# First attention of a two-layer transformer: values in two halves, each behind its half of the rounds, and keys and values of the next group half an iteration later

## The chip, the core and the metric

The kernel runs on one core of a Trainium2 chip. The metric is the device time of one execution in microseconds (us). Engines are named as in the profile: PE is TensorE's matmul stream and PEld its weight loads, DVE is VectorE, ACT is ScalarE, POOL is GpSimd, SP issues most DMAs. Everything is fp32.

## What is computed

64 sequences `x` of 128 rows and width 128 go through two blocks of attention and experts, each with a residual sum:

```python
x = x + xattn0(layernorm(x), fside, ctx, ctx, ...)   # keys: 128 of fside @ Wk, and 120 raw ctx rows
x = x + ffn0(layernorm(x), wqkv, w1, w2)             # top 2 of 8 experts, attention router
x = x + xattn1(layernorm(x), ctx, ctx, ...)          # 120 keys
x = x + ffn1(layernorm(x), Wg, bg, W1, W2)           # top 2 of 8 experts

def xattn0(x1, x2, mem_k, mem_v, ...):               # 16 heads of 8
    q = x1 @ Wq + bq
    k = concat(x2 @ Wk + bk, mem_k); v = concat(x2 @ Wv + bv, mem_v)
    out = softmax(q k^T / sqrt(8)) v                 # per head, 248 keys
    return out @ Wp + bp
```

The first attention (`xattn0`) is the part that matters here: 64 x 16 heads of a 128 x 248 score matrix.

## The kernel before, in words

**Loops.** `attention()` (L232) is run once for each layer; `first` is true for the first. It is a software pipeline over `it` = 0 to 68 (L553): in one iteration different sequences stand at different stages. `on(back, f)` runs a step for sequence `it - back`. In the first attention, iteration `it` does:

1. `rounds(0, 1)`: in each round two banks of row maxima for sequence `it` (`max_bank`, matmuls L394, then a DVE reduction L414) and two banks of transposed scores for sequence `it - 2` (`score_bank`, L430, then an exp on ACT, L438). All 32 matmuls of a pair of rounds work on 32 rows of the PE array, four at a time. Rounds 0 and 1 take the maxima of heads' half 0 and the scores against the 128 computed keys; rounds 2 and 3 the maxima of half 1 and the scores against the 120 context keys.
2. `out4` (output projection, L511, of `it - 5`), `shift` (two transposes L459 of the maxima of `it - 1`, and two DVE operations L462 that put them into the queries), `out5` (residual sum L516 and statistics L109).
3. `aside.ahead` (statistics of a later sequence) and `aside.call`: the router of the first experts, which works for two groups at a time in small pieces. One `call` is made here and one more ahead of the second pair of rounds. Its pieces are DVE operations (L718 to L774, L820 to L861), some on ACT and POOL, and on PE transposes (L176), logits (L681, copied by DVE in L685) and counts (L831, which waits for DVE's L820).
4. `values(it - 3, 0)`, `values(it - 3, 1)` and `out1`: probabilities times values, L475, on 32 columns of the PE array; each half is 16 matmuls (32 records in the profile, as each fp32 matmul has two). Both halves write one bank, and `out1` copies its 256 columns (ACT, L484).
5. `context` (in one iteration of four), `prep(it, 0)`, the second `aside.call`.
6. `rounds(2, 3)`.
7. `out3` (transpose L504, ACT copy L506) of `it - 4`, `out2` (two transposes L491, then DVE's L495 and L497) of `it - 3`, `prep(it, 1)`, `aside.end` (DMAs of zeros, each behind L495).

**Groups.** Four sequences make a group; keys, values and queries are prepared for a whole group, one group ahead. With `j = it % 4`, `prep(it, half)` does:

- `j` = 0: `prep_q` in both halves. The matmul L292 and two ACT writes L301 come in half 0, two more writes from the same bank in half 1.
- `j` = 1: nothing. In these iterations the router has its transposes and logits on PE.
- `j` = 2: `prep_v` (four matmuls L214, DVE adds L221) in half 0, `prep_k` (matmul L202, two ACT writes L207) in half 1.
- `j` = 3: `prep_x` in half 1 (transposes L176, ACT copy L177).

`context` loads 2 x 240 KB of context keys (L261) and 960 KB of context values (L266) for the next group, into the slot of the group before. `prep_v` writes the values of that slot too, so both must come after the last `values` of the old group, which stand at `j` = 2.

**Order.** PE, ACT, DVE and POOL run in the order of the program text (`tc.manual_schedule(engines=ORDERED)`); only SP's queue is put in order by the planner.

**Banks.** `mtile()` takes one of eight PSUM banks. A new tile gets the bank that was given back first, and a bank is given back behind its last reader in program order. So the tile number n waits for the reader that gave back number n - 8. In a pair of rounds the order is maximum, score, maximum, score, for each round. A bank that is held over other work (that of `prep_q`, from half 0 to half 1) leaves seven for what comes between. The last bank of rounds 2 and 3 at `j` = 0 is therefore the first bank of the same pair, behind its reduction.

Of the kernel before, what the change touches and what calls it, by code (L numbers as in the profile page):

```python
# [8 lines left out]
F32 = mybir.dt.float32  # L9
# [9 lines left out]
GB = 4  # L19
NG = B // GB  # L20
S = 128
# [3 lines left out]
NV = 2  # L25
# [19 lines left out]
def transformer_kernel(ctx, tc, a, out):  # L45
    nc = tc.nc
# [46 lines left out]
    rows = ctx.enter_context(tc.tile_pool(name="rows", bufs=2))  # L93
# [91 lines left out]
    for s in range(2):  # L185
        k = keep.tile([128, NV, GB, KF + KC], F32, name=f"k2_{s}", tag=f"k2_{s}")
        K2.append(k)
        v = keep.tile([KF, GB, H // 2, 2, 32], F32, name=f"v_{s}", tag=f"v_{s}")
# [23 lines left out]
    def values_of(w, src, g, n0, pv):  # L212
        for j in range(GB):
            nc.tensor.matmul(  # L214
                pv[:n0, j * D : (j + 1) * D], lhsT=src[:, j, :], rhs=w["wv"],
                start=True, stop=True,
            )
        pv5 = pv[:n0, :].rearrange("k (b h i d) -> k b h i d", b=GB, i=2, d=HD)
        bv5 = w["bv"][:n0, :].rearrange("k (h i d) -> k h i d", i=2, d=HD)
        for i in range(2):  # L220
            nc.vector.tensor_tensor(  # L221
                VS[g % 2][0][:n0, :, :, i, 16 * i : 16 * i + HD], pv5[:, :, :, i, :],
                bv5[:, :, i, :].unsqueeze(1).to_broadcast([n0, GB, H // 2, HD]),
                ALU.add,
            )
# [6 lines left out]
    def attention(layer, w, norm, first, aside):  # L232
# [5 lines left out]
        with ExitStack() as es:  # L238
# [5 lines left out]
            if first:  # L244
                for s in range(2):
                    v = work.tile([128, GB, H // 2, 2, 32], F32, name="vc", tag="vc")
# [4 lines left out]
            src, q4s, xnTs, ps_, pavs, pts, ots, normed = {}, {}, {}, {}, {}, {}, {}, {}  # L251
# [7 lines left out]
            def context_k(g):  # L259
                for v in range(NV):  # L260
                    nc.sync.dma_start(  # L261
                        k2[g % 2][:, v, :, KF:], a["ctx_k"][:, v, g * GB : (g + 1) * GB, :]
                    )

            def context_v(g):
                nc.sync.dma_start(  # L266
                    vs[g % 2][1].rearrange("k b h i w -> k b (h i w)"),
                    a["ctx_v"][:, g * GB : (g + 1) * GB, :],
                )

            def context(g):
                if first:
                    context_k(g)
                    context_v(g)

            def mtile():
                return banks.tile([128, 512], F32, name="bank", tag="bank")
# [28 lines left out]
            def prep_k(g):  # L306
                keys_of(w, src[g], g, n0, mtile())
# [9 lines left out]
            def prep_v(g):  # L317
                values_of(w, src[g], g, n0, mtile())
# [20 lines left out]
            def prep(it, half):  # L339

                g, j = it // GB + 1, it % GB
                if not first:
                    if g == 1:
                        if (j, half) == (0, 0):
                            prep_k(1)
                            prep_v(1)
                        elif (j, half) == (0, 1):
                            prep_x(1)
                        elif j == 1:
                            prep_q(1, half)  # L350
                            if half:
                                prep_heads(1)
                    elif g < NG:
                        pieces = (
                            (), (lambda: prep_k(g), lambda: prep_heads(g)),
                            (lambda: prep_v(g), lambda: prep_x(g)),
                            (lambda: prep_q(g, 0), lambda: prep_q(g, 1)),
                        )[j]
                        if half < len(pieces):
                            pieces[half]()  # L360
                    return
                if half == 0 and it < GB - 1:
                    prep_batch(it + 1)
                if (it, half) == (0, 1):
                    prep_v(0)
                    norm_of(1)
                if (it, half) == (1, 1):
                    biased(0)
                if (it, half) == (2, 1):
                    prep_x(1)  # L370
                if (it, half) == (3, 0):
                    prep_q(1, 0)
                    prep_q(1, 1)
                if (j, half) == (3, 1):
                    if g + 1 < NG:
                        prep_x(g + 1)
                elif g >= NG:
                    return
                elif j == 0 and it:
                    prep_q(g, half)  # L380
                elif (j, half) == (2, 0):
                    prep_v(g)
                elif (j, half) == (2, 1):
                    prep_k(g)


# [78 lines left out]

            def values(b, v):
                g, j = divmod(b, GB)
                if v == 0:
                    pavs[b] = mtile()
                pav = pavs[b]  # L470
                p = ps_[b]
                for i in range(2):
                    for c, (_, n) in enumerate(chunks):
                        for ra in range(4):
                            nc.tensor.matmul(  # L475
                                pav[32 * ra : 32 * ra + 32, v * S : (v + 1) * S],
                                lhsT=vs[g % 2][c][:, j, 4 * v + ra, i, :],
                                rhs=p[:n, c, ra, (2 * v + i) * S : (2 * v + i + 1) * S],
                                start=(i == 0 and c == 0), stop=(i == 1 and c == nc_ - 1),
                            )  # L480

            def out1(b):
                ov = rows.tile([128, NV * S], F32, name="ov", tag="ov")
                nc.scalar.copy(ov, pavs.pop(b)[:, : NV * S])  # L484
                ots[b] = ov

            def out2(b):
                ov = ots.pop(b)
# [30 lines left out]
            def norm_of(g):  # L519
                if g < NG:  # L520
                    normed[g] = norm.normed(g)
                    biased(g)
# [30 lines left out]
            for it in range(B + 5):  # L553
                def on(back, *steps):
                    b = it - back
                    if 0 <= b < B:
                        for f in steps:
                            f(b)

                def rounds(*which):  # L560
                    ba = it if it < B else None
                    bc = it - 2 if 0 <= it - 2 < B else None
                    for r in which:
                        if ba is not None or bc is not None:
                            round_(ba, bc, r)

                if first and it % GB == 2:
                    norm_of(it // GB + 2)
                if 2 <= it <= B + 1 and it - 2 not in ps_:
                    ps_[it - 2] = work.tile([128, nc_, 4, 512], F32, name="p", tag="p")  # L570
                if it % GB == 0 and 0 < it // GB + 1 < NG:
                    if it:
                        loads(it // GB + 1)
                vals = (lambda b: values(b, 0), lambda b: values(b, 1), out1)
                if first:
                    rounds(0, 1)


                    on(5, out4)
                    on(1, shift)  # L580
                    on(5, out5)
                    aside.ahead(it)
                    aside.call(it, mtile)
                    on(3, *vals)
                    if it % GB == 2 and it // GB + 1 < NG:
                        context(it // GB + 1)
                    prep(it, 0)
                    aside.call(it, mtile)
                    rounds(2, 3)
                    on(4, out3)  # L590
                    on(3, out2)
                    prep(it, 1)
                    aside.end(it, work, mtile)
                else:
                    on(3, *vals)
                    rounds(0, 1)


                    aside.piece(mtile)
                    prep(it, 0)  # L600
                    on(4, out3)
                    on(3, out2)
                    on(5, out4)
                    aside.call(it, mtile)
                    prep(it, 1)
                    on(1, shift)
                    on(5, out5)
                    aside.ahead(it)
                    if it > GB and it % GB == 1:
                        norm_of(it // GB + 1)  # L610
                    aside.fetch_for(it)
                    aside.call(it, mtile)
                ps_.pop(it - 3, None)
                yield
# [951 lines left out]
```

## Time and profile before

| | |
|---|---|
| median of 3 runs | 1522.33 us (1518.69 to 1523.64) |
| profiled execution | 1516.1 us, of which 1514.3 us are the span of the trace |
| granted PE clock, mean | 0.989 |
| first attention's loop | about 20 to 615 us of the span |
| experts of the first layer, second attention with its experts | about 615 to 965 us, 965 to 1514 us |
| iterations 33 to 40, start of L459 to start of L459 | 320.0 to 394.9 us: 74.9 us for eight |

Work repeats every eight iterations, because the router takes two groups at a time. Times within the trace are from the start of the span. A line of the timeline has the start, the length, engine, line, operation, output and inputs, shapes, count, and in brackets the idle time of the engine ahead of it and what ended it. A line of the waits has who waited for whom, the sum in us, how often, and the longest.

### The profile page before, as it was taken

How to read it: one execution, taken by the hardware profiler on the slowest of the kernel's cores; microseconds unless marked ns; L12 is line 12 of the kernel's file. 1: busy time of each engine (PE TensorE's matmuls, PEld its weight loads, DVE VectorE, ACT ScalarE, POOL GpSimd, SP SyncE). 2: the span in 40 equal slices, each digit the busy share in tenths (PEclk: the TensorE clock that was granted, in tenths of full speed). 3: DMA queues.
4: the chain of work that ended last, by engine and by line, in shares of the span. 5: the costliest groups of instructions: out<-in, count | busy, mean ns of one | idle time of the engine just before them, and what ended most of it. 6: DMA issues, size and time to landing. Idle time of an engine off the chain costs nothing.

```text
span 1514.3 us, 42033 instructions
## 1 busy us (share of the span) xinstructions
PE 1421.0 (94%) x16620; PEld 1107.5 (73%) x16620; DVE 1102.4 (73%) x3024; ACT 847.6 (56%) x1740; POOL 640.4 (42%) x1195
## 2 busy tenths in 40 slices
PE   7999999999999999888999999898999999999987
PEld 5777777777777677777888888566666776767665
DVE  6777888888888988455754444687777778787763
ACT  4666666666666666543333333566667566666643
POOL 4123254646465635654001122377546555454210
PEclk9999999999999999999999999899999999999999
DMA  8433333333222221366766667111011111100000
GB/s 201 120 80 80 79 82 96 89 93 94 63 66 60 58 73 40 107 184 202 214 197 199 201 195 205 49 34 34 22 36 29 39 35 32 31 29 23 8 16 22
DMA packets 143719, 133.03 MB, mean 88 GB/s; under 512 B 48546, under 2 KB 126114, under 8 KB 141602
## 3 DMA queue, kind: packets, MB, share of 16 engines
q1 hardware_dynamic: 135330, 113.02, 27.3%
q0 software_dynamic: 8192, 17.32, 3.7%
q8 instruction: 132, 2.16, 0.6%
q14 instruction: 65, 0.53, 0.1%
HBM read 97.32 MB, written 32.97 MB: 86 GB/s over the span
## 4 chain that ended last, share of the span: by engine, by line
PE 69%; DVE 15%; DMA 4%; POOL 4%; ACT 4%; issue 2%; SPq 1%; POOLq 0%; DVEq 0%; ACTq 0%
PE bank L430 11%; PE bank L394 10%; PE bank L475 9%; PE bank L1115 9%; PE bank L1424 4%; PE bank L1445 4%; DVE nm L414 4%; PE bank L1128 3%; DMA q<-xs 2%; PE bank L407 2%; PE bank L214 2%; DVE q L462 2%; PE bank L511 2%; PE bank L681 2%; PE bank L202 2%
## 5 line engine op out<-in xcount | busy, mean ns | idle before, releaser
L414 DVE TENSOR_REDUCE nm<-bank 128x2 f32<-128x496 f32 (+1 forms) x768 | 463.5, 662 | 77.6 <-PE bank L430 61.8
L438 ACT ACTIVATE p<-bank 120x512 f32<-120x512 f32 (+1 forms) x768 | 402.1, 605 | 126.8 <-PE bank L430 123.9
L430 PE MATMUL bank<-q,k 32*120 32x256 f32 (+1 forms) x3072 | 438.1, 399 | 11.4 <-DVE nm L414 5.2
L430 PEld LDWEIGHTS bank<-q,k 32*120 32x120 f32 (+1 forms) x3072 | 293.5, 181 | 56.8 <-DVE nm L414 17.3
L394 PE MATMUL bank<-k,q 32*128 32x248 f32 x2048 | 291.0, 399 | 0.7 <-ACT q L334 0.5
L394 PEld LDWEIGHTS bank<-k,q 32*128 32x128 f32 x2048 | 202.2, 189 | 47.9 <-issue 11.0
L1120 DVE TENSOR_TENSOR p<-p,bank 128x256 f32<-128x256 f32 x213 | 88.0, 420 | 121.0 <-ACT p L1119 120.5
L475 PE MATMUL bank<-p,v 128*32 128x128 f32 (+1 forms) x4096 | 175.6, 275 | 0.2
L407 PE MATMUL bank<-k,qf 32*128 32x480 f32 x512 | 153.8, 602 | 0.8 <-ACT qf L295 0.8
L807 POOL DMA_INDIRECT xs<-xn,at x128 | 129.2, 1009 | 27.9 <-issue 24.3
L1119 ACT ACTIVATE p<-bank 128x256 f32<-128x256 f32 x213 | 81.0, 384 | 98.9 <-PE bank L1115 97.9
L484 ACT COPY ov<-bank 128x256 f32<-128x256 f32 x128 | 48.1, 376 | 143.5 <-PE bank L475 143.4
L475 PEld LDWEIGHTS bank<-p,v 128*32 128x32 f32 (+1 forms) x4096 | 108.8, 109 | 22.8 <-issue 13.7
L1364 POOL DMA_INDIRECT yb<-ys,back x112 | 108.5, 969 | 27.7 <-issue 19.5
L1115 PE MATMUL bank<-q 128*128 128x256 f32 x516 | 118.6, 379 | 1.6 <-ACT q L1106 1.6
L462 DVE SCALAR_TENSOR_TENSOR q<-bank,c_smask,q 128x256 f32<-128x256 f32 x256 | 111.1, 475 | 8.2 <-PE bank L459 7.8
L167 POOL TENSOR_SCALAR xn<-x,mv,rstd 128x128 f32<-128x128 f32 x252 | 110.2, 449 | 7.5 <-issue 1.4
L1115 PEld LDWEIGHTS bank<-q 128*128 128x128 f32 x516 | 94.7, 190 | 13.0 <-ACT q L1106 1.9
L475 PE MATMUL bank<-p,vc 120*32 120x128 f32 x2048 | 103.2, 272 | 0.0
L155 POOL TENSOR_SCALAR rstd<-mv 128x4 f32<-128x4 f32 x32 | 6.3, 198 | 219.9 <-DVE mv L113 123.0
L301 ACT ACTIVATE q<-bank,c_a_bq,c_hmask 128x512 f32<-128x512 f32 x124 | 90.1, 789 | 9.8 <-PE bank L292 9.8
L1157 POOL DMA_INDIRECT kvT<-ys,back x16 | 15.4, 961 | 189.7 <-DMA vc<-xs 114.0
(224 smaller groups left out, 2465.7 us busy)
## 6 DMA issues: line engine op xcount, KB each, us to landing
q<-in_w SPq DMA_DIRECT2D x43, 576.0 KB
vc<-in_w SPq DMA_DIRECT2D x28, 576.0 KB
vc<-in_ctx_v SPq DMA_DIRECT2D x16, 960.0 KB
ys<-zero SPq DMA_DIRECT2D x71, 128.0 KB
k<-in_ctx_k SPq DMA_DIRECT2D x32, 240.0 KB
q<-xs SPq DMA_DIRECT2D x43, 128.0 KB
ys<-q SPq DMA_DIRECT2D x43, 128.0 KB
x<-in_x SPq DMA_DIRECT2D x16, 256.0 KB
```

The source lines that it names most:

```text
L167: nc.gpsimd.tensor_scalar(xn[:, j, :D], xg[g][:, j, :], self.mv[:, b, 0:1], self.rstd[:, b : b + 1], ALU.add, ALU.mult,)
L301: nc.scalar.activation(q4s[g][:, :, s, :], pq.rearrange("p (b q) -> p b q", b=GB), AF.Identity, bias=w["bq"][:, s : s + 1], scale=hmask[:, ...
L394: nc.tensor.matmul(pa[:, u, :], lhsT=q4s[g][r, j, s, :], rhs=k2[g % 2][r, s // 2, j, :], start=True, stop=True,)
L407: lambda: nc.tensor.matmul(pa, lhsT=qfs[g][r, j, :], rhs=k4s[g][r, :, j, :], start=True, stop=True),
L414: nc.vector.tensor_reduce(nm[b % 2].rearrange("q i (a s) -> q a i s", s=16)[:, 2 * ra + v : 2 * ra + v + len(slots) // 2, :, 0], pa.rearra ...
L430: nc.tensor.matmul(pb[:n, v * 256 : (v + 1) * 256], lhsT=k2[g % 2][r, v, j, k0 : k0 + n], rhs=q4s[g][r, j, 2 * v : 2 * v + 2, :].rearrange ...
L438: nc.scalar.activation(ps_[b][:n, c, ra, :], pb[:n], AF.Exp, scale=SCALE)
L462: nc.vector.scalar_tensor_tensor(q, pm, smask[:, v : v + 1], q, ALU.mult, ALU.add)
L475: nc.tensor.matmul(pav[32 * ra : 32 * ra + 32, v * S : (v + 1) * S], lhsT=vs[g % 2][c][:, j, 4 * v + ra, i, :], rhs=p[:n, c, ra, (2 * v + ...
L807: s = nc.gpsimd.indirect_dma_start(xs, bass.IndirectOffsetOnAxis(at[:, j, k : k + 1], 0), xn, None)
L1115: nc.tensor.matmul(ph[:, u, :], lhsT=w[:, c, u * 128 : (u + 1) * 128], rhs=xT, start=True, stop=True)
L1364: nc.gpsimd.indirect_dma_start(y[:, k, b % 2, :], None, ys, bass.IndirectOffsetOnAxis(back[:, b, k : k + 1], 0),)
```

## The change

- `half_out(b, v)` computes one half of the values into a bank of its own and copies its 128 columns into the half of a common tile `ov`. Half 0 stands where the whole values stood, half 1 behind `rounds(2, 3)`. `out1` isn't used in the first attention any more.
- `context` and `prep_v` for the next group move behind half 1, `prep_k` moves from half 1 of `prep` into half 0, where `prep_v` was.
- `prep(it, 1)` moves ahead of `out2`, so that `prep_x`'s transposes and the second two writes of `prep_q` stand between `out3` and `out2`.

The second attention keeps its order.

```diff
@@ -379,8 +379,6 @@
                 elif j == 0 and it:
                     prep_q(g, half)
                 elif (j, half) == (2, 0):
-                    prep_v(g)
-                elif (j, half) == (2, 1):
                     prep_k(g)
@@ -465,7 +463,7 @@
             def values(b, v):
                 g, j = divmod(b, GB)
-                if v == 0:
+                if v == 0 or first:
                     pavs[b] = mtile()
@@ -483,6 +481,14 @@
+            def half_out(b, v):
+
+                values(b, v)
+                if v == 0:
+                    ots[b] = rows.tile([128, NV * S], F32, name="ov", tag="ov")
+                cols = slice(v * S, (v + 1) * S)
+                nc.scalar.copy(ots[b][:, cols], pavs.pop(b)[:, cols])
@@ -581,15 +587,17 @@
                     on(5, out5)
                     aside.ahead(it)
                     aside.call(it, mtile)
-                    on(3, *vals)
-                    if it % GB == 2 and it // GB + 1 < NG:
-                        context(it // GB + 1)
+                    on(3, lambda b: half_out(b, 0))
                     prep(it, 0)
                     aside.call(it, mtile)
                     rounds(2, 3)
+                    on(3, lambda b: half_out(b, 1))
+                    if it % GB == 2 and it // GB + 1 < NG:
+                        context(it // GB + 1)
+                        prep_v(it // GB + 1)
                     on(4, out3)
+                    prep(it, 1)
                     on(3, out2)
-                    prep(it, 1)
                     aside.end(it, work, mtile)
```

## The prediction

> **What bounds the kernel now.** I read the page first, then the stretches of 100 us, then the waits of the first attention, then the timelines of PE and DVE for a few of its iterations.
>
> ```profile
> PE 1421.0 (94%) x16620; PEld 1107.5 (73%) x16620; DVE 1102.4 (73%) x3024; ACT 847.6 (56%) x1740; POOL 640.4 (42%) x1195
> ```
> ```profile
> 300.00:400.00 100.00, 98.67 (x1545) 75.09 (x1543) 86.08 (x215) 65.15 (x132) 55.83 (x126) 1.00 0.30 80
> ```
> Columns of the second: length, then PE, PEld, DVE, ACT, POOL busy us, clock, DMA share, GB/s. In the first attention (20 to 615 us, the only place that the change touches) PE looks full at the full clock and DVE stands at 86%. The ends of matmuls are modelled, so I measured PE from start to start:
>
> ```profile
> 361.40 0.47 PE L394 MATMUL bank<-k,q 32*128 32x248 f32 x1
> ...
> 363.31 0.33 PE L504 MATMUL bank<-ident,o 128*128 128x128 f32 x1
> ```
> ```profile
> 326.14 0.47 PE L394 MATMUL bank<-k,q 32*128 32x248 f32 x1
> ...
> 328.91 0.38 PE L511 MATMUL bank<-c_a_wo,oT 128*128 128x128 f32 x1
> ```
> Both are the same 32 matmuls. A pair of rounds that waits for nothing takes 363.31 - 361.40 = 1.91 us; the other takes 2.77. Call rounds 0 and 1 the first pair, 2 and 3 the second, and `it` mod 4 the position. From 100 to 500 us the first pair takes 2.77, 2.66, 2.41, 2.96 at positions 2, 3, 0, 1, so it stalls 0.86 + 0.75 + 0.50 + 1.05 = 3.16 us in each four iterations; the second is clean except at position 0 (2.92) and 2 (2.03 to 2.09). The waits name the cause:
>
> ```profile
> DVE nm L414 <- PE bank L430: 42.8, 84, 2.0
> PEld bank L504 <- DVE nm L414: 14.4, 37, 2.4
> PEld bank L430 <- DVE nm L414: 14.4, 36, 1.6
> ```
> PE waits for banks that DVE's reductions give back, and DVE in its turn waits for PE: eight banks tie two nearly full engines together. DVE between two pairs:
>
> ```profile
> 346.93 1.83 DVE L414 TENSOR_REDUCE nm<-bank 128x2 f32<-128x496 f32 x3
> 348.67 0.87 DVE L462 SCALAR_TENSOR_TENSOR q<-bank,c_smask,q 128x256 f32<-128x256 f32 x2
> 349.46 0.28 DVE L516 TENSOR_TENSOR x<-x,bank 128x128 f32<-128x128 f32 x1
> 349.77 0.49 DVE L109 BATCH_NORM_STATS2 st<-x 128x6 f32<-128x128 f32 x2
> 350.18 0.22 DVE L841 COPY flat<-counts 128x64 f32<-128x64 f32 x1
> ...
> 351.31 0.23 DVE L855 TENSOR_TENSOR row<-row,start 128x64 f32<-128x64 f32 x1
> 352.21 1.26 DVE L414 TENSOR_REDUCE nm<-bank 128x2 f32<-128x496 f32 x2 [0.67 <-PE bank L430]
> 353.68 1.26 DVE L414 TENSOR_REDUCE nm<-bank 128x2 f32<-128x496 f32 x2 [0.22 <-PE bank L394]
> ```
> Everything that DVE owes besides reductions, up to the router's steps, lies between the first pair and the second; after the second come only L495 and L497 (0.25 + 0.29). The whole values stand in the same middle, and give DVE time there.
>
> **The change, part by part.** Clock of one iteration from the start of its first pair, DVE on time: reductions start at 1.13 and then every 0.585, the last at 2.89; shift, x and statistics follow, and the router's first step starts 2.10 after the last reduction's start (348.09 to 350.18), at 4.98. A clean second pair needs DVE 1.13 after its own start. PE: first pair 1.91, out4 0.33, shift 0.31, values.
>
> *Values in halves.* Whole values are eight groups in 1.90 us (0.22 each, the last 0.33 to the next kind of work). A half is 0.24 + 2 x 0.22 + 0.33 = 1.01, two 2.02: +0.12 an iteration. The trace has no pair directly ahead of values; I take nothing for that crossing, bounds 0 and +0.11 (the loss seen on leaving values). The Trainium skill ("TensorEngine Tiling (Array Packing)", Key Properties) says that a change of tiling mode drains TensorE; it names no time. It speaks against this change: rounds work on 32 rows, values on 32 columns, so by the rule the unseen crossing has a drain as well, and if that were again 0.11, the sum would rise by 64 x 0.11 = 7 us.
>
> *The middle is 0.89 us shorter for PE.* The second pair could start at 1.91 + 0.64 + 1.01 = 3.57 plus what preparation stands there. DVE isn't that early:
> - Position 1 (transposes 0.53, router matmuls 1.00, first pair 2.35 because its seventh bank comes from the q writes): second pair from 5.44. DVE does 1.35 to 1.72 of router steps from 4.98, then the logits' copy L685 (0.26), whose bank is the pair's last: 6.96 in one group, 6.61 in the next. Last bank + about 1.1 = 8.10 and 7.74 instead of 7.35: +0.75 and +0.39.
> - Position 2: prep_k's matmul (1.06) now stands right ahead of the second pair, whose last bank is the key bank; L207's two writes end 2.6 after the matmul's start (334.98 to 337.59). The pair ends at 7.30, not 6.53: +0.77. The same stall of 0.75 leaves the first pair of position 3.
> - Position 3: in every second group L831 waits for L820 on DVE.
>
> ```profile
> 341.06 0.21 DVE L820 TENSOR_TENSOR m<-one,one 128x64 f32<-128x64 f32 x1
> ```
> ```profile
> 341.42 0.41 PE L831 MATMUL bank<-m,c_upper 128*128 128x64 f32 x2
> ```
>   L820 starts at 4.98 whatever PE does, so L831 stays at 5.34; PE would reach it at 3.85: +1.49. In the other group L768 (0.67) makes the reductions 0.6 late, and the second half, whose bank is the one that the first reduction gives back, waits from 5.76 to 6.30: +0.54.
> - Position 0: the q bank is held over the second pair, so its last bank is that of its own first reduction. DVE is busy until 4.98 + 1.36 (L841 to L855), or + 1.64 (L771 to L727); the pair ends at 8.13 or 8.41, clean 6.51: +1.62 and +1.90.
>
> *The second half behind the second pair.* It fills the time in which the first pair stalled. Left there are 0.44 at position 1 (q writes) and 0.29 at position 3 (L497, late behind L221). But out2 now needs a copy of values just computed: half start + 1.15 (as 340.90's end to L484) + 0.30 (copy of 128x128, L506) + 0.06, against 1.01 + 0.17 of PE work: +0.33 at positions 1 and 0; elsewhere prep_v or prep_x covers it.
>
> *Two copies for one.* ACT +0.22 (2 x 0.30 for 0.373); ACT is at 65% and the second copy is in the 0.33 above. The Trainium skill ("Perfetto Trace Analysis", Optimizing Scalar/DVE Operations) says breaking up instructions may finish work sooner where ScalarE isn't full but causes bubbles; that would let the first half's copy end 0.07 sooner; no wait above ends with L484, so by the trace it wins nothing.
>
> *prep_v behind the second half.* Its 1.09 moves on PE; L221's two adds (0.78) leave the middle of position 2 for the place ahead of L495, counted in the 0.29. prep_v and prep_x no longer stand right ahead of a pair: about -0.14 and -0.09. The context loads: the keys' DMA must wait for the last scores of the group before anyway (issued 325.39, needed by the pair at 345.06); the DMA busy share falls from 1.09 at 327 to 329 us to 0.31 after. Half an iteration (4.5 us) is covered by some 15 us. If the SP queue put them behind the 960 KB of context values, the cover would be about 5. Cost 0.
>
> **Sum for eight iterations.** On: 1.14 + 2 x 0.77 + 1.49 + 0.54 + 3.52 + 2 x (0.44 + 0.29) + 4 x 0.33 + 8 x 0.12 = 12.0. Off: first pairs 2 x 3.16, second pairs 2 x 1.01 + 0.12 + 0.18, L831's wait today 0.18, out2's small waits 0.3, prep_v and prep_x 0.5: 9.6. Net +2.3 on 74.9. Iterations 9 to 58 carry the router: 6.25 x 2.3 = +14.4. Iterations 5 to 8 have none; there DVE is ready at 4.98, and the same steps give 7.8 + 9.7 + 7.7 + 9.3 = 34.5 for the 35.5 seen: -1. The last six, bare of preparation, give 7.5 for 7.75: -1. Two iterations stall 0.9 and 2.0 today on long DVE lists (second pair 3.80 and 4.08); with less cover I add 1.5, an estimate. Total +14 us: 1516.1 (span 1514.3) becomes 1530. The median shown, 1522.33, lies 6.2 above that execution: **1536**.
>
> **Rivals.**
> - *Faster: the halves do balance.* If late reductions don't reach PE, as in iterations 5 to 8, each four iterations win 0.9: 15 x 0.9 = 13, 1509. For it: the first pair's 3.16 is real, and ends wherever 0.95 us of other work stands ahead of it. Against: DVE idles only 0.4 to 1.1 us in the middle today, less than the 0.89 taken away at most positions, and L820, L685 and the first reduction are on PE's path. It decides from where DVE's router steps in the middle are 0.3 us (4.98 less 3.57 + 1.13) shorter than PE's preparation there; of the eight positions that holds at one, position 2 of the second group (L763, 0.67, beside prep_k's 1.06). Chance 0.17.
> - *No difference.* The terms at positions 0 and 3 are half as large, because a late reduction is partly made up by the next: 2.8 less in eight, 6.25 x 2.8 = 17 us less, 1519. For it: today's second pair at position 0 stalls 1.01 only. Against: its last bank hangs on the first reduction, with nothing in between. Chance 0.15.
> - *Much slower: the key load is late.* Some 2 us more at each of 14 groups' first pair: 1564. Against: the 15 us above. Chance 0.05.
> - The forecast, 1525 to 1550: 0.63. Its width: each "+" above rests on DVE rows that repeat within 0.1, but 0 to 0.11 for the new crossing (up to +7) and stalls that hide each other (up to -10) are open.
>
> **Numbers.** Faster means below 1517.8 (0.3%, about what a measurement of this kernel can tell from no change), slower above 1526.9: 0.17, 0.15, 0.68. The range 1512 to 1552 leaves out most of the first rival and the third.
>
> **What would show it.** Right: first pairs near 1.9 to 2.4; second pairs of 2.3 to 3.8, longest at position 0; L831 still right behind L820; PE waiting at the second half for L414, and L491 for L484; DVE's share of the stretch down by 2 to 3 points. Wrong: second pairs near 1.91 outside position 0, or an iteration group under 37 us (it is 37.4 now).

## The result, and the profile after

The change takes 1527.38 us (median of 20 runs, 1521.83 to 1533.40), the kernel before beside it 1522.28 (20 runs, 1514.61 to 1523.74): a ratio of 1.0035, 95% interval 1.0022 to 1.0047. A second comparison (E11) gave 1.0054, 1.0034 to 1.0073. The change is slower by 5 to 9 us, where 14 were forecast. The profiled execution of the change is its slowest, 1533.4 us; so sizes below are measured inside the trace, from one start of the shift (L459 before, L457 after) to the next, and not from the two spans. Line numbers of the change are 2 lower than before up to the values (L392 maxima, L428 scores, L412 their reduction, L473 values) and 6 to 8 higher behind them (L497 the transposes of `out2`, L839 the counts); L491 is the copy of a half.

Below are the busy time of the engines from the page of the change, and then its row for 300 to 400 us (length, then PE, PEld, DVE, ACT, POOL busy us with instructions, clock, DMA share, GB/s):

```profile
PE 1414.6 (92%) x16620; PEld 1097.1 (72%) x16620; DVE 1101.7 (72%) x3024; ACT 861.0 (56%) x1804; POOL 642.4 (42%) x1195
```
```profile
300.00:400.00 100.00, 94.62 (x1500) 71.27 (x1497) 85.32 (x212) 66.97 (x141) 53.79 (x120) 1.00 0.33 88
```

PE was 98.67 us busy in this stretch and is 94.62; DVE was 86.08 and is 85.32. Only ACT has more to do (two copies for one: +1.8 us there). PE waits more, at the full clock. The waits over the whole trace say for whom, before and then in the change:

```profile
PEld bank L430 <- DVE nm L414: 17.3, 44, 1.6
...
PEld bank L475 <- DVE nm L414: 2.9, 17, 0.2
```
```profile
PEld bank L473 <- DVE nm L412: 22.8, 69, 1.4
...
PEld bank L428 <- DVE nm L412: 19.4, 18, 2.8
...
PEld bank L497 <- ACT ov L491: 11.8, 35, 1.1
```

Values that wait for a bank which a reduction gives back (L475, now L473) have gone from 2.9 us in 17 waits to 22.8 in 69. Of the scores' waits for such a bank (L430, now L428) there are 18 and not 44, but their sum has risen from 17.3 us to 19.4 and the longest from 1.6 to 2.8. The long ones stand at position 0. The third row, `out2` waiting for the copy of the second half, is as good as new. PE at position 0 of the change, from the start of a second pair on:

```profile
389.22 0.47 PE L392 MATMUL bank<-k,q 32*128 32x248 f32 x1
...
391.84 0.47 PE L428 MATMUL bank<-q,k 32*120 32x256 f32 x1 [1.06 <-DVE nm L412]
...
392.89 0.43 PE L473 MATMUL bank<-p,v 128*32 128x128 f32 x8
```

The second pair takes 392.89 - 389.22 = 3.67 us (2.92 before), the half right behind it 1.02, the next first pair 2.43 (2.96 before). The last bank of the second pair waits for the pair's own first reduction, and that stands behind the router on DVE. First before, where the same steps of the router end in time and DVE then waits for PE (the pair starts at 388.26 there); then the change:

```profile
388.78 0.22 DVE L727 TENSOR_REDUCE m<-r 128x8 f32<-128x64 f32 x1
389.39 1.26 DVE L414 TENSOR_REDUCE nm<-bank 128x2 f32<-128x496 f32 x2 [0.40 <-PE bank L430]
```
```profile
389.57 0.67 DVE L779 TENSOR_REDUCE r<-pp 128x64 f32<-128x512 f32 x1
390.15 0.54 DVE L781 RECIPROCAL r<-r 128x64 f32<-128x64 f32 x1
390.73 0.22 DVE L782 TENSOR_TENSOR r<-r,r 128x64 f32<-128x64 f32 x1
390.99 0.22 DVE L735 TENSOR_REDUCE m<-r 128x8 f32<-128x64 f32 x1
391.12 1.25 DVE L412 TENSOR_REDUCE nm<-bank 128x2 f32<-128x496 f32 x2
```

The reduction could have started 1.13 behind 389.22, at 390.35; the router's steps hold it until 391.12. At position 3 of every second group the first half ends early and then nothing can go on, because the counts need DVE's L828 (start 342.88):

```profile
341.43 0.40 PE L473 MATMUL bank<-p,vc 120*32 120x128 f32 x8
343.24 0.41 PE L839 MATMUL bank<-m,c_upper 128*128 128x64 f32 x2 [1.40 <-DVE s L756]
```

(The releaser named, L756, is the operation behind L828.) Summed over iterations 33 to 40 from start to start, before against after: first pairs 21.59 to 16.93 us (-4.66), second pairs 17.59 to 21.17 (+3.58), values with the waits behind them 15.37 to 17.76 (+2.39), `out2` 2.98 to 3.44 (+0.46), the rest -0.55: 74.9 to 76.1, +1.2.

E1 to E7 and E10 were measured while the kernel before itself took 1569 to 1571 us, with single stalls of some 1.4 us that five of these kernels, repeated as E12 to E16 beside a kernel before of 1520 us, don't show; E2, E5 and E6 have no repeat.

### The profile page after: what moved, and what is told of

Its sections match the earlier page's. It is cut to its first block, busy times and chain, and to the rows that moved or that the text cites. A ratio compares the mean times of both kernels' runs of the same rounds, so it can differ in the third digit from the quotient of the medians.

```text
span 1531.4 us, 42138 instructions
## 1 busy us (share of the span) xinstructions
PE 1414.6 (92%) x16620; PEld 1097.1 (72%) x16620; DVE 1101.7 (72%) x3024; ACT 861.0 (56%) x1804; POOL 642.4 (42%) x1195
## 3 DMA queue, kind: packets, MB, share of 16 engines
q8 instruction: 131, 2.15, 0.6%
## 4 chain that ended last, share of the span: by engine, by line
PE 61%; DVE 22%; ACT 6%; DMA 5%; POOL 3%; issue 2%; SPq 1%; POOLq 0%; DVEq 0%; ACTq 0%
PE bank L1123 9%; PE bank L428 8%; PE bank L473 8%; DVE nm L412 7%; PE bank L392 6%; PE bank L1432 4%; PE bank L1453 4%; PE bank L1136 3%; DVE q L460 3%; DMA q<-xs 3%; PE bank L405 2%; PE bank L214 2%; ACT p L436 2%; PE bank L497 2%; PE bank L202 2%
## 5 line engine op out<-in xcount | busy, mean ns | idle before, releaser
L412 DVE TENSOR_REDUCE nm<-bank 128x2 f32<-128x496 f32 (+1 forms) x768 | 460.9, 661 | 56.7 <-PE bank L428 42.1
L428 PE MATMUL bank<-q,k 32*120 32x256 f32 (+1 forms) x3072 | 421.5, 396 | 19.4 <-DVE nm L412 12.7
L428 PEld LDWEIGHTS bank<-q,k 32*120 32x120 f32 (+1 forms) x3072 | 291.6, 181 | 60.3 <-DVE nm L412 19.4
L392 PE MATMUL bank<-k,q 32*128 32x248 f32 x2048 | 268.0, 394 | 0.7 <-ACT q L334 0.5
L392 PEld LDWEIGHTS bank<-k,q 32*128 32x128 f32 x2048 | 189.1, 189 | 40.0 <-DVE x L522 20.5
L473 PE MATMUL bank<-p,v 128*32 128x128 f32 (+1 forms) x4096 | 179.1, 280 | 4.5 <-DVE nm L412 4.3
L473 PEld LDWEIGHTS bank<-p,v 128*32 128x32 f32 (+1 forms) x4096 | 105.2, 110 | 48.9 <-DVE nm L412 22.8
L473 PE MATMUL bank<-p,vc 120*32 120x128 f32 x2048 | 103.5, 273 | 0.0
L138 POOL TENSOR_TENSOR mv<-st 128x4 f32<-128x4 f32 x31 | 6.4, 207 | 202.2 <-DVE st L109 202.2
```

Of the source, the lines that this page charges most:

```text
L392: nc.tensor.matmul(pa[:, u, :], lhsT=q4s[g][r, j, s, :], rhs=k2[g % 2][r, s // 2, j, :], start=True, stop=True,)
L412: nc.vector.tensor_reduce(nm[b % 2].rearrange("q i (a s) -> q a i s", s=16)[:, 2 * ra + v : 2 * ra + v + len(slots) // 2, :, 0], pa.rearra ...
L428: nc.tensor.matmul(pb[:n, v * 256 : (v + 1) * 256], lhsT=k2[g % 2][r, v, j, k0 : k0 + n], rhs=q4s[g][r, j, 2 * v : 2 * v + 2, :].rearrange ...
L473: nc.tensor.matmul(pav[32 * ra : 32 * ra + 32, v * S : (v + 1) * S], lhsT=vs[g % 2][c][:, j, 4 * v + ra, i, :], rhs=p[:n, c, ra, (2 * v + ...
```

## The experiments

**Theory (place).** What costs the change time is DVE's work ahead of the second pair, above all the router's second call. The halves bring PE to that pair 0.9 us earlier and DVE not at all. **Rivals:** the split itself costs (more instructions, a second copy, crossings); the moves of keys, of the values' preparation and of `out2` cost; any late DVE operation costs both kernels the same.

| kernel | ratio to before | 95% interval | iterations 33 to 40, us | iterations 9 to 56, us |
|---|---|---|---|---|
| before (E9) | | | 74.9 | 452.5 |
| change (E11) | 1.0054 | 1.0034 to 1.0073 | 76.1 | 456.0 |
| split alone, in the middle (E15) | 0.9996 | 0.9978 to 1.0013 | 74.9 | 452.4 |
| moves alone (E16) | 0.9987 | 0.9969 to 1.0005 | 75.2 | 451.0 |
| before, router later (E13) | 0.9950 | 0.9926 to 0.9973 | 74.0 | 445.1 |
| change, `prep(it, 0)` first (E14) | 0.9978 | 0.9962 to 0.9993 | 75.3 | 452.9 |
| change, router later (E12) | 0.9881 | 0.9863 to 0.9899 | 72.9 | 438.2 |
| both of these (E8) | 0.9807 | 0.9787 to 0.9828 | 71.1 | 429.9 |

### The two kernels again (E9, E11)

No edit.

> The kernel before, unchanged, for a profile on the chip of the next three runs. In its first profile iterations 33 to 40 take 74.9 us and iterations 9 to 56 take 451.5. If the stalls of 1.3 to 1.5 us that the experiments showed in every second group at position 2 (E1's second pair of 3.37 us against 1.91 in the other group) belong to the chip or to its clock, this profile has them too, and iterations 33 to 40 take 75.5 to 76.5 us. If they belong to the kernels tried, the eight iterations take 74.9 us as in the first profile.

> The change, unchanged, on the same chip as E3 and E8, so that their differences to it carry no difference of chips. By the first comparison it takes 1.0035 of the kernel before (0.35% more), iterations 33 to 40 take 76.1 us in its profile against 74.9. If the change depends on the chip more than the kernel before does, since its second halves leave less room for a late copy, the ratio rises to 1.006 to 1.010 and the surplus over 76.1 us lies in waits of the out2 transposes (L497) and of the reductions (L412).

Eight iterations take 74.90 and 76.13 us: both as in the first profiles, to 0.02. The change's ratio is 1.0054, and its interval overlaps the first one's (1.0034 to 1.0073, 1.0022 to 1.0047); of the 8.7 us between the medians the loop, from iteration 1 to 64, shows 592.1 - 587.2 = 4.9. In both profiles of the change the loop takes 592.1, so no new wait of any size has come in.

### The split alone (E1, E15)

```diff
                     aside.call(it, mtile)
-                    on(3, *vals)
+                    on(3, lambda b: half_out(b, 0), lambda b: half_out(b, 1))
```

> Both halves stand in the middle, each with its own bank and copy; everything else as before. Theory (place): the change costs because half of the values leaves the middle, where DVE needs the time; the split by itself costs only PE's extra crossing, 0.12 to 0.14 us in each of 64 iterations, so at most +9 us on before (1522.3), iterations 33 to 40 at 75.4 to 76.0 us (74.9 before, 76.1 after), first pairs still stalled by 2.4 to 3.0 us and no wait of out2 for a copy. Rival (split): the loss of the change is the split alone, wherever the second half stands: then this equals the change, +5 us, with the place neutral. Rival (keys): the loss comes from prep_k in the middle: then 1522, no loss.

> E1 again: the kernel before with values in two halves, both in the middle. On a chip without the extra stalls eight iterations take 74.9 us or up to 0.5 more, and the ratio lies between 0.999 and 1.003. If the extra 1.4 us of E1's second pairs at position 2 were the work of the split and not of the chip, eight iterations take 76.4 us again.

E1: 1.0000 (0.9985 to 1.0015), with second pairs of 3.37 us in every second group at position 2. E15: 0.9996, and there 2.03 and 2.09, as before. The two halves take 1.90 us together, as the whole values do. So two banks and two copies (266 ns each, where the whole takes 373) neither cost nor win anything where they stand, and the first rival falls. A half takes 1.02 in the change only because other work follows each.

### The moves alone (E4, E16)

Whole values stay in the middle; `prep_k`, `context` with `prep_v` and `prep(it, 1)` go where the change has them.

> The values are whole and in the middle as before; prep_k in half 0, context and prep_v behind the second pair and prep(it, 1) ahead of out2 as in the change. Theory (place): the key bank's stall moves from the first pair of position 3 to the second pair of position 2, prep_v's adds make L497 late for the first pair of position 3 by 0.4; about -0.2 us in four iterations, -3 us, 1519. Rival (keys): the moves make the loss: +5 us, 1527. Rival (split): 1522.

> E4 again: the kernel before with only the moves of the keys, the values' preparation and out2. If E4's stalls were the chip's, eight iterations take 74 to 75.5 us, and the ratio lies between 0.997 and 1.003: the moves alone neither win nor lose much, and the change's loss is that of the second half's new place. Rival: the moves alone cost as much as the change, 1.0035 to 1.0054 and 76 us.

E4: 1.0007 (0.9990 to 1.0024). E16: 0.9987, eight iterations 75.2: the second pair at position 2 stalls as in the change (2.66), the counts come as late as in the change (2.49 from the start of the values, 2.08 before; they are L830 here, and wait for L819, the L828 of the change), and the first pairs at position 3 give back 0.46 each (2.20 for 2.66). The second rival falls: the moves cost 0.3 us in eight iterations, and nothing that the time shows.

### The key bank back (E2), and further ahead (E7, E14)

E2 puts `prep_k` of the change back into half 1, and all of `prep(it, 1)` with it behind `out2`. E7 and E14 put `prep(it, 0)` ahead of the first half:

```diff
-                    on(3, lambda b: half_out(b, 0))
                     prep(it, 0)
+                    on(3, lambda b: half_out(b, 0))
```

> The change, but prep_k is back in half 1 of prep, behind out2. Theory (place): prep_k's 1.06 us in the middle of position 2 give DVE time; without them the second pair there starts at 3.57, DVE is ready at 6.0, and the key bank stalls the first pair of position 3 again: about +1.0 us in each four iterations on the change, 15 groups, 1527.4 + 15 = 1542. Rival (keys): the 0.75 us that the second pair of position 2 waits for the key bank are what the change loses: without them -11 us, 1516. Rival (split): no difference to the change, 1527.

> The change, with prep(it, 0) ahead of the first half of the values and not behind it. Theory: L207's two writes of the keys begin 1.02 us earlier against the second pair, whose last bank is the key bank, so the second pair of position 2 falls from 2.66 to 2.1 us; position 0 stays at 3.4 to 3.7, since its last bank hangs on its own first reduction; 15 x 0.55 = -8 us on the change, -3 on before. Rival: that pair waits for DVE's reductions and not for the key bank: no difference to the change, +5 on before.

> E7 again: the change with prep(it, 0) ahead of the first half. E8 gained 1.7 us in eight iterations over E12 by this step, where the router stood later. Place theory: the key bank's stall of 0.75 us at position 2 goes here too, but the router's second call still stands ahead of the pair: 0.7 to 1.5 us less in eight iterations than the change's 76.1, 4 to 9 us less in all, 0.998 to 1.003 of the kernel before. Rival, from E7: nothing is won, 1.0035 to 1.0054 as the change.

E2: 1.0155 (1.0135 to 1.0176). It has no repeat, and E7, measured beside it, stands 0.7% above its own repeat; with as much taken off, E2 is at about 1.0085 (an estimate), still above the change. So the change doesn't get faster when its key bank goes back: the new place of `prep_k` is no loss. E7: 1.0048 (1.0030 to 1.0067), a miss for the theory. E14: 0.9978, eight iterations 75.3. The second pair at position 2 goes from 2.66 to 2.15 in one group and 2.50 in the other: the key bank's wait goes, and the router's DVE steps take half its place (in the second group one that itself waits for POOL and holds the first reduction until 361.90):

```profile
361.30 0.69 DVE L771 TENSOR_REDUCE r<-pp 128x64 f32<-128x512 f32 x1 [0.64 <-POOL pp L769]
```

From iteration 9 to 56 E14 wins 3.1 us on the change, and 1.0 in iterations 5 to 8, which have no router. Another 5.2 us lie in iterations 1 to 4 (35.7 for 40.9), but E6, which does there what the change does, takes 36.4: that part isn't shown to be the work of the edit.

### One more DVE operation ahead of the second pair (E5, E6)

To the kernel before (E5) and to the change (E6), an unused reduction of 0.6 us is added in iterations 9 to 63:

```diff
                     aside.call(it, mtile)
+                    if 8 < it < B:
+                        nc.vector.tensor_reduce(pad, lw1, AX.X, ALU.max)
                     rounds(2, 3)
```

> The kernel before, with one more DVE operation (a reduction of 512 columns, about 0.585 us of DVE) ahead of the second pair of rounds in iterations 9 to 63. It computes nothing that is used. Theory (place): in the middle of the kernel before DVE idles 0.4 to 1.1 us, since the whole values stand there, so the operation is mostly covered: +0.1 us an iteration, +0 to +8 us on before. Rival (split): DVE's place makes no difference between the two kernels, so this one and the change pay the same.

> The change with the same unused DVE operation ahead of the second pair in iterations 9 to 63. Theory (place): the middle has no DVE idle time left at positions 0 and 1 and in one of two groups at positions 2 and 3, so the operation is paid nearly whole: 55 x 0.45 = +25 us (between +18 and +32) on the change, that is +30 on before. Rival (split): the same increment as in the kernel before.

E5: 1580.24 us, 1.0056 (1.0035 to 1.0076), so 8.9 us for 55 operations. E6: 1608.17 us, 1.0269 (1.0215 to 1.0324), so 36.9 us above before. That isn't all the operation's: 5 to 9 are the change's own, and the change wasn't measured beside E6. E7, which differs from the change only in the place of `prep(it, 0)`, stood 0.7% above its repeat there, 11 us. That leaves 17 to 21 us (an estimate) of 55 x 0.585 = 32, some 0.35 an operation for 0.16 in E5. The pairs show it directly. Position 0 of E6, where the router's list ends with the added line (L595), which holds the reduction (L413 here):

```profile
362.33 0.68 DVE L595 TENSOR_REDUCE pad<-c_lw1T 128x1 f32<-128x512 f32 x1
362.93 1.25 DVE L413 TENSOR_REDUCE nm<-bank 128x2 f32<-128x496 f32 x2
```
```profile
363.64 0.47 PE L429 MATMUL bank<-q,k 32*120 32x256 f32 x1 [1.37 <-DVE nm L413]
```

The second pair there takes 3.97 and 4.27 for the change's 3.38 and 3.67: +0.6, all of it (E2, with the stalls of E6's occasion and no such operation, has 3.41 and 3.68). At position 3 (3.02 for 2.43) too; at position 2 (2.66 to 2.72) next to nothing, as there the key bank is later still. In E5 the same operation adds 0 to 0.1 at position 0, nothing at position 1 and 0 to 0.2 at position 3, where whole values cover it, and 0.6 at position 2 of one group. The rival "the same for both" falls, and at position 0 "a late reduction is partly made up by the next" with it.

### The router's second call later (E3, E12; E10, E13; E8)

E3 and E12 are the change with the second call behind the second half; E10 and E13 the kernel before with it behind the second pair; E8 is E12 with `prep(it, 0)` ahead of the first half.

```diff
                     prep(it, 0)
-                    aside.call(it, mtile)
                     rounds(2, 3)
                     on(3, lambda b: half_out(b, 1))
+                    aside.call(it, mtile)
```

> The change, but the second call of the router stands behind the second half of the values and not ahead of the second pair, so that L831 and L685 are off the way to the second pair, and about half of DVE's router steps leave the middle. Theory (place): L831's wait (1.47 in every eighth iteration) goes, second pairs at position 0 lose 0.4 to 0.8 us, at position 1 the change of sign is open (its logits' 1.00 us leave the middle too): -2 us in eight iterations, five and a half eights, 1527.4 - 11 = 1516. Rival (split): no difference beyond 2 us, 1527, since no copy and no crossing is touched.

> E3 again (the change, with its second router call behind the second half instead of ahead of the second pair), now beside the change and the kernel before on one chip. Place theory (what costs the change time is the router's VectorE work that now stands right ahead of a second pair that TensorE reaches half a product earlier): 0.988 to 0.993 of the kernel before, 1.0 to 1.5% under the change, and second pairs of position 0 under 3 us. Rival (a chance of that chip): within 0.3% of the kernel before.

E3: 0.9907 (0.9885 to 0.9928). E12: 0.9881, 1502.63 us, 1.7% under the change. The row for 300 to 400 us, and position 0 on DVE and PE:

```profile
300.00:400.00 100.00, 97.64 (x1560) 73.60 (x1563) 88.44 (x226) 68.90 (x147) 60.32 (x135) 1.00 0.31 82
```
```profile
375.71 0.67 DVE L779 TENSOR_REDUCE r<-pp 128x64 f32<-128x512 f32 x1
376.55 1.26 DVE L412 TENSOR_REDUCE nm<-bank 128x2 f32<-128x496 f32 x2 [0.18 <-PE bank L428]
378.03 1.26 DVE L412 TENSOR_REDUCE nm<-bank 128x2 f32<-128x496 f32 x2 [0.22 <-PE bank L392]
379.20 0.54 DVE L781 RECIPROCAL r<-r 128x64 f32<-128x64 f32 x1
```
```profile
377.29 0.47 PE L428 MATMUL bank<-q,k 32*120 32x256 f32 x1 [0.31 <-DVE nm L412]
```

The same list is now cut in two: L779 ahead of the pair, L781 and its successors behind it, and the first reduction waits for PE and not for them. The bank's wait is 0.31 instead of 1.06, and the pair takes 2.92 us as before. Of the 3.3 us that eight iterations win on the change, 1.5 are the counts' wait, 1.1 the second pairs and 0.5 the waits of `out2`. At position 3 the counts follow the second half without a wait:

```profile
333.27 0.43 PE L839 MATMUL bank<-m,c_upper 128*128 128x64 f32 x2
```

Does the router's place alone do it?

> The kernel before (whole values in the middle), with the router's second call behind the second pair of rounds. Theory (place): in the kernel before DVE has idle time in the middle and is late behind the second pair; moving router steps there makes it later, so the first pair stalls as before: within 4 us of before. Rival: the gain of 0.9% that the change showed with a later second call comes from the router's place alone, whatever the values do: then about -0.9% here as well, 1508.

> E10 again: the kernel before, with its second router call behind the second pair. On a chip without the extra stalls: by the place theory the kernel before loses little to the router's place, because whole values stand in its middle; its own second pairs stall only at position 0 (1.01 us, twice in eight iterations) and 2 (0.15), so eight iterations go from 74.9 to 73 to 74.5 us, and the ratio to the kernel before lies between 0.992 and 0.998, against 0.988 with the halves (E12). Rival: the router's place is all that matters and the halves add nothing; then it takes 0.988 of the kernel before as E12 does.

E10: 0.9954 (0.9934 to 0.9974). E13: 0.9950. So no: less than half of E12's gain. With whole values in the middle the router's steps behind the second pair make the first pair late, as only `out3`, `out2` and at most some preparation stand between. DVE of E13 behind a second pair at position 1, whose next first pair takes 3.03 us (2.77 before):

```profile
322.29 0.25 DVE L685 COPY lg<-bank 128x96 f32<-128x96 f32 x1
322.45 0.25 DVE L495 RECIPROCAL rs<-bank 128x16 f32<-128x16 f32 x1
322.73 0.29 DVE L497 TENSOR_TENSOR o<-bank,rs 128x128 f32<-128x128 f32 x1
322.94 2.41 DVE L414 TENSOR_REDUCE nm<-bank 128x2 f32<-128x496 f32 x4
```

In E12 the second half stands in that gap. The change by itself loses 0.4 to 0.5%, the router's place by itself wins 0.5%, both together 1.2%. In eight iterations the change costs 1.2 us while the router stands ahead of the second pair (74.9 to 76.1), and wins 1.2 once it stands behind it (74.05 in E13 to 72.85 in E12): here PE's work and DVE's had to be divided over the same two gaps.

> E3 with prep(it, 0) ahead of the first half as well. In E3 the key bank's two reductions and copies at position 2 still follow the middle on TensorE, and the second pair waits for them. Place theory: the key bank's stall of 0.75 us in each of the two groups of eight iterations goes, so 6.25 x 1.5 = 9 us at most and 0.25 to 0.6% under E3. Rival, from E7 (where the same step left the change's time as it was): the wait behind it, for the first pair's reductions, takes its place, and the time is E3's within 0.2%.

E8: 0.9807 (0.9787 to 0.9828), 1489.68 us (5 runs, 1486.92 to 1495.41), 1.9% under before and 2.5% under the change. Over E12 eight iterations win 1.7 us, where the key bank had held 1.5. Its row of the same stretch:

```profile
300.00:400.00 100.00, 97.31 (x1610) 75.69 (x1610) 90.27 (x232) 69.84 (x148) 59.80 (x132) 1.00 0.35 91
```

DVE is 90% busy now, and the stretch holds 1610 of PE's records where it held 1545. The expectation's rival, that another wait takes its place, holds only while the router stands ahead of the pair (E14).

## Why the prediction was right in its direction and too large

**Bound and mechanism: right.** In iterations 33 to 40 second pairs of 2.05 to 3.67 (2.3 to 3.8 forecast), longest at position 0, but for the one behind the counts; first pairs of 1.91 to 2.44; L839 right behind L828; the second half waiting for reductions, and `out2` for the second copy. Second pairs of 1.91, named as a sign of being wrong, stand from iteration 17 to 48 only at position 3 behind the counts, where the sum itself has a clean pair, and once at position 1 (iteration 21). DVE's share of the stretch fell by 0.8 points, not by 2 to 3, as the loss is smaller. E6 and E12 show the mechanism by adding to it and taking from it.

**The step that failed is "Iterations 9 to 58 carry the router: 6.25 x 2.3 = +14.4".** Both factors were too large. From iteration 9 to 58 the loop got longer by 3.6 us (E9 to E11; 4.5 in the first profiles), not by 14.4 + 1.5. The rest of the loop's 4.9 us is +0.4 in iterations 1 to 4, -1.1 in 5 to 8 and +2.1 from 59 on, where a win had been forecast: part of the loss that was found came from a term with the wrong sign, which is luck.

- *The 2.3* is a small difference of two large sums, 12.0 and 9.6; measured they are about 11.1 and 9.9, so 1.2. No term is off by more than 0.25 us: position 1 +0.53 and +0.14 for 0.75 and 0.39 (the pair starts 0.08 later, behind a first pair of 2.43 for 2.35, and its end lies 0.15 earlier: the copy L693 that holds the last bank ends 0.1 sooner than I had added up), position 0 +1.47 and +1.76 for 1.62 and 1.90, the waits of `out2` 0.24 for 0.33. Right within 0.03: the key bank (0.75 for 0.77), the counts (1.47 for 1.49), the other group at position 3 (0.52 for 0.54, the second half's wait for the first reduction). What was taken off came to 0.3 more. Misses of 0.1 to 0.25 in a few terms, nearly all to one side, halved the result.
- *The 6.25.* Iterations 9 to 13 have the router's matmuls, and of its DVE steps only the copy of the logits: in the trace of before, DVE between two pairs shows only L462, L516, L109, L221 and L685 there, and the next step, L763, starts at 146.34, in iteration 14. So iterations 9 to 16 went from 74.2 to 73.1 us like the four without a router, where 2.3 were added. The stage starts at 9 on PE, and at 14 on DVE, where its cost is.
- *Long lists* (+1.5): one more miss, of the sign. Second pairs are 5.04 for 3.81 us at iteration 52 and 2.82 for 1.91 at 53, but the list that stalled iteration 54 (12.0 and 13.0 us in the two profiles of before) is done by then: the iteration takes 10.0. With them iterations 49 to 56 moved by +0.5 in the first profiles and by -0.4 from E9 to E11.
- *The last six* (-1): +2.1. I took them to be bare; but the router's DVE steps run there to iteration 63 (L776 at 608.09 in the trace of the change), and L839 waits once more at 59 (9.1 for 8.3 us).
- *Iterations 5 to 8* (-1): -1.1, and their pieces as forecast (7.75, 9.71, 7.69 and 9.27 us from first pair to first pair).

**The unseen crossing, rounds to values: 0 was right.** A second pair with a half right behind it takes 1.90 us at position 3 (343.80 to 345.70 in the trace of the change), as a clean pair with a transpose behind it (1.91). The Trainium skill ("TensorEngine Tiling (Array Packing)", Key Properties) says that changing the tiling mode drains TensorE. Both pairs end in such a change, so these starts don't show whether there is a drain, only that the step to the values costs no more than the step to a transpose. **The copies** came out as weighed, too: E15 has them alone, at no gain and no cost.

**The rivals.** *Faster* lost because its condition, DVE's middle shorter than PE's, holds where the router's steps are absent: 1.1 us less in iterations 5 to 8, and 1.1 in 9 to 16. E12 takes the router's second call out of DVE's middle, and with it the faster kernel comes true, 17 us under before (medians). *No difference* is out, as the interval begins at 1.0022; its reason (a late reduction partly made up) is refuted by E6's +0.60 at position 0. *Key load late*: the pairs that first use the new keys, the first pairs at position 0, take 1.91 to 1.93 us from iteration 12 to 56 and show no wait for it.

**Still open:** how the 8.7 us of E11's medians and the loop's 4.9 go together. From iteration 64 to the end, nearly all of it code that the change doesn't touch, the trace of E9 takes 911.3 us and that of E11 914.7; the two profiles of before differ there by 3.2 us and those of the change by 4.1, so the rest may be chance, but no run shows it. And the sizes of E2 and E6, for want of a repeat.

## What to carry to other kernels

Where two in-order engines hand each other buffers, work that is taken out of one gap may have to be matched on the other: here, dividing TensorE's products over two gaps lost 0.4 to 0.5% while VectorE's list stayed in one, and won 1.2% once that list was divided as well, 1.9% with the key bank filled earlier too. A forecast that is the difference of two sums several times its size needs terms much closer than the 0.1 to 0.25 us by which some were off here, or a range that says so; and how many iterations a cost has is to be counted on the engine that causes it.

## What was not expected of the hardware

- The same program shows a stall in one trace that it doesn't have in another. At position 2 of every second group the second pair of E1 takes 3.37 us and that of E15, the same kernel, 2.03, both at a granted clock of 1.00 from 300 to 400 us. In E1's trace VectorE's L221 starts 1.38 us behind the end of the matmuls that fill its bank (L214), and ScalarE's copy L493 1.70 behind those of its own (L475); in E15's it is 0.04 and 0.07. From iteration 64 to the end, nearly all of it code that no edit touches, E1 takes 953 us and E15 910. The cause is open.
